# An attention and feed-forward block: each tile's chain spread over three loop periods, with the 32-column matmul groups of three tiles placed in a row

## Chip, cores and metric

The kernel runs on one core of a Trainium2 chip. The metric is the device time of one execution in microseconds. Before the change the median of three runs is 1268.93 us (1268.37 to 1269.41).

## What is computed

The input x is 128 sequences of 32 positions with 512 features, all f32. In the reference's own words, cut to what matters:

```python
def _L0_cond_ref(x, condition, weights):           # one 32x32 matrix per sequence
    return jnp.einsum('bct,bcd->bdt', x, weights[condition])

def _L0_attn_ref(h, w_qkv, q_ln_w, q_ln_b, k_ln_w, k_ln_b, w_out):   # 32 heads of 16
    qkv = jnp.clip(jnp.einsum('bsd,ed->bse', h, w_qkv), -8, 8)
    q, k, v = jnp.split(qkv, 3, axis=-1)
    q, k = _layer_norm(q, q_ln_w, q_ln_b), _layer_norm(k, k_ln_w, k_ln_b)
    ...
    scores = jnp.where(causal, scores * HEAD_DIM ** -0.5 + alibi_bias, -jnp.inf)
    attn = jnp.einsum('bhqk,bkhd->bqhd', jax.nn.softmax(scores, axis=-1), v)
    return jnp.einsum('bsd,ed->bse', attn, w_out)

def _L0_cond2_ref(x, weight, adapter_ids):         # one 512x512 adapter per sequence
    return jnp.einsum('bsi,boi->bso', x, weight[adapter_ids])

def _L0_ffn_ref(h, gate_w, up_w, down_w, fc1_w, fc2_w, expert_w, ln_gamma, ln_beta):
    routing, _ = jax.lax.top_k(h @ gate_w, 2)
    shared = (jax.nn.relu(h @ up_w) ** 2) @ down_w
    routed = (((h @ fc1_w) @ expert_w) * routing.sum(-1, keepdims=True)) @ fc2_w
    return _layernorm(shared + routed, ln_gamma, ln_beta)

x = x + _L0_attn_ref(_L0_cond_ref(x, ...), ...)
x = x + _L0_ffn_ref(_L0_cond2_ref(x, ...), ...)
```

The scale of the scores, the bias and the mask are folded together in the second function; nothing else is.

## The kernel before

The 4096 rows are cut into 32 tiles of 128 rows, four sequences each. Tiles go two by two (`GRP = 2`) through the wide layers of the feed-forward part, since their weights are then loaded into the array once for 256 columns. All weights but the adapters stay on chip. The routed experts' three matrices are multiplied together once, in the prologue (`routed_inner`, `routed_outer`).

A tile t goes through these steps. The name in brackets is how the profile calls the result.

- `load`: x[t] by DMA from SP, and the rows of its conditioning matrices (cw) by an indirect DMA from GpSimd. `load_adapters`: eight DMAs of 512 KB from SP (adw), into a pool of eight buffers, so those of tile t wait until the matmuls of tile t-1 have read theirs.
- `mix`: GpSimd spreads cw into a block-diagonal matrix (blk, L205); four matmuls apply it (pxc, L213); ScalarE copies the result (xcT, L218).
- `project(t, i)`: q, k or v (pqkv, L230), four matmuls of 512 columns each; VectorE clips it and takes the statistics of q and k (L236 to L243).
- `normalise`: ScalarE's square root, then VectorE (L153, L155, L249). `turn`: q and k are transposed. Tiles 0 to 3 do it on TensorE (`flat`, pt, L291); all others (`swap`) by VectorE's transpose in 32x32 blocks (blocks_qk, L272), one DMA to DRAM (away_qk) and four back (T_qk). `scale`: ScalarE applies the norms' weights to k and q (L312, L326) and VectorE spreads k over the heads (kx, L316).
- `scores`: matmuls with 64 rows and 32 columns of the array (psc, L340); VectorE adds the bias (s, L347). `exponent`: VectorE's maximum, GpSimd's subtraction, ScalarE's exp (L357, L358, L363). `share`: sum, reciprocal, and GpSimd's product (L368 to L371). `flip`: VectorE transposes the weights (pT, L379).
- `spread`: GpSimd lays v out per sequence (vx, L390). `weigh`: matmuls with 32 columns of the array (po, L403); VectorE transposes (aT, L414). `attend`: the output projection (pw, L423), added to x (L427).
- `turn_x`: x transposed. Tiles 0 to 2 do it on TensorE with a ScalarE copy (pt_x, L434), all others by `swap`. `adapt`: matmuls with 32 columns of the array (pad, L453); VectorE writes the pair's hT (L458).
- `route(t, half)`: the gate and the merged routed experts (pr, L472), scaled on ScalarE (y, L483, L485) by the sum of the two best gates (top, gs, VectorE).
- `up(g, f)`: eight per pair (pu, L492), ScalarE's relu (act, L497), squared by GpSimd (L498). `down(t, quarter)`: four per tile (pd, L506). `total`, `finish`: the sum, the layer norm and the second residual, then the store.

The main loop runs over periods t. In an even period the eight calls of `fill` are the `up`s of the pair before; in an odd one they are the `down`s of its two tiles. Around them, in the order of the code, one period holds: mix(t+1), scores(t), exponent(t), the projections of q and k of t+1 with share(t) and flip(t) between, normalise and turn of t+1, two or three fills with route(t-2, 0), weigh(t), route(t-2, 1), attend(t), turn_x(t), the projection of v of t+1, the other fills with spread(t+1) and scale(t+1), and adapt(t) last. So a tile's chain lies in two periods: the projections in one, and all from the scores to the adapters in the next.

This order is written by hand, but it is not the queues' order in every place. TensorE's queue holds it as written. On the other engines the framework that builds the program lays the instructions down by when it expects their operands: in the trace, the ScalarE part of scale(t+1) stands ahead of that of finish, which comes earlier in the code, and VectorE's kx alternate with the steps of total. Each engine then works its queue in that order. Buffers come from pools: `w1` has one of each kind, `w2` two, `xp` six tiles of x, and all matmul results share eight PSUM banks.

```python
        when(more, mix, t + 1)
        when(here, scores, t)
        when(here, exponent, t)
        ...
        when(here, weigh, t)
        ...
        when(t % GRP, total, g * GRP + 1)
        when(here, adapt, t)
    finish(NTILE - 1)
```

Of the kernel before, what the change touches and what calls it, by code (L numbers as in the profile page):

```python
# [11 lines left out]
F32 = mybir.dt.float32  # L12
# [5 lines left out]
P = 128  # L18
# [23 lines left out]
def adaln_attn_ffn(  # L42
# [27 lines left out]
    def bank(name):  # L70
        return ps.tile([P, 512], F32, tag="ps", name=name)
# [37 lines left out]
    down_sb = const.tile([P, FC, D], F32, name="down_sb")  # L109
    gam_sb = const.tile([P, D], F32, name="gam_sb")  # L110
    bet_sb = const.tile([P, D], F32, name="bet_sb")
    xp = ctx.enter_context(tc.tile_pool(name="xp", bufs=6))
    wp = ctx.enter_context(tc.tile_pool(name="wp", bufs=8))
    w1 = ctx.enter_context(tc.tile_pool(name="w1", bufs=1))
    w2 = ctx.enter_context(tc.tile_pool(name="w2", bufs=2))
# [14 lines left out]
    def routed_inner(l):  # L130
        pe2 = bank(f"pe2_{l}")
        for m in range(LC):
            nc.tensor.matmul(  # L133
                pe2, lhsT=exp_t[:, m, ts(l, P)], rhs=fc2_t[:, m, :],
                start=(m == 0), stop=(m == LC - 1),
            )
        nc.scalar.copy(e2[:, l, :], pe2)
# [20 lines left out]
    def load(t):  # L158
        x_t = xp.tile([P, D], F32, tag="x", name=f"x_{t}")
        nc.sync.dma_start(out=x_t, in_=x[ts(t, P), :])  # L160
        cw = sm.tile([P, S], F32, tag="cw", name=f"cw_{t}")
        nc.gpsimd.indirect_dma_start(
            out=cw,
            out_offset=None,
            in_=cond_w,
            in_offset=bass.IndirectOffsetOnAxis(ap=rows[:, t : t + 1], axis=0),
        )
        tiles[t] = {"x": x_t, "cw": cw}
# [29 lines left out]

    def mix(t):

        s = tiles[t]
        blk = w2.tile([P, SEQ, S], F32, tag="blk", name=f"blk_{t}")
        nc.gpsimd.tensor_tensor(  # L205
            out=blk,
            in0=s["cw"].unsqueeze(1).broadcast_to([P, SEQ, S]),
            in1=m_seq.unsqueeze(2).broadcast_to([P, SEQ, S]),
            op=ALU.mult,
        )  # L210
        pxc = bank(f"pxc_{t}")
        for c in range(DC):
            nc.tensor.matmul(  # L213
                pxc[:, ts(c, P)], lhsT=s["x"][:, ts(c, P)],
                rhs=blk.rearrange("p a b -> p (a b)"), start=True, stop=True,
            )
        s["xcT"] = w1.tile([P, DC, P], F32, tag="xcT", name=f"xcT_{t}")
        nc.scalar.copy(s["xcT"].rearrange("p c n -> p (c n)"), pxc)  # L218

    def project(t, i, chunks=range(DC)):  # L220

        s = tiles[t]
        if chunks[0] == 0:
            if i == 0:
                s["qk"] = w2.tile([P, 2, D], F32, tag="qk", name=f"qk_{t}")
                s["v"] = w2.tile([P, D], F32, tag="v", name=f"v_{t}")
                s["mv"] = sm.tile([P, 2, 2], F32, tag="mv2", name=f"mv_{t}")
            s["pp", i] = bank(f"pqkv_{t}_{i}")
        for c in chunks:
            nc.tensor.matmul(  # L230
                s["pp", i], lhsT=s["xcT"][:, c, :], rhs=wqkv_sb[:, c, ts(i, D)],
                start=(c == 0), stop=(c == DC - 1),
            )
        if chunks[-1] < DC - 1:
            return
        nc.vector.tensor_scalar(  # L236
            out=s["qk"][:, i, :] if i < 2 else s["v"], in0=s["pp", i],
            scalar1=-CLIP, scalar2=CLIP, op0=ALU.max, op1=ALU.min,
        )
        if i < 2:  # L240
            st = sm.tile([P, 6], F32, tag="st", name=f"st_{t}_{i}")
            nc.vector.bn_stats(out=st, in_=s["qk"][:, i, :])
            nc.vector.bn_aggr(out=s["mv"][:, i, :], in_=st)  # L243
# [21 lines left out]
    def swap(srcs, name):  # L265


        n = len(srcs)
        blocks = w1.tile([P, DC, n, DC, S], F32, tag=f"blocks{n}", name=f"blocks_{name}")
        out = (w1 if n == 1 else w2).tile([P, SEQ, n, DC, S], F32, tag=f"T{n}", name=f"T_{name}")  # L270
        for k, src in enumerate(srcs):
            last_flip[:] = [nc.vector.transpose(  # L272
                out=blocks[:, :, k], in_=src.rearrange("p (c i d) -> p i c d", c=DC, i=DC)
            )]
        away = dram.tile([SEQ, S, DC, n * P], F32, tag=f"away{n}", name=f"away_{name}")
        nc.sync.dma_start(
            out=away.rearrange("j d i n -> (j d) (i n)"),
            in_=blocks.rearrange("p i k c n -> p (i k c n)"),
        )
        for i in range(DC):  # L280
            nc.sync.dma_start(
                out=out[ts(i, S)].rearrange("p j k c n -> p j (k c n)"),
                in_=away[:, :, i].rearrange("j d n -> d j n"),
            )
        return out
# [8 lines left out]
    def turn(t):  # L294


        s = tiles[t]
        if t < 2 * GRP:
            s["T"] = w2.tile([P, SEQ, 2, DC, S], F32, tag="T2", name=f"T_qk_{t}")
            s["raw"] = [flat(s["qk"][:, i, :], f"{t}_{i}") for i in range(2)]  # L300
        else:
            s["T"] = swap([s["qk"][:, i, :] for i in range(2)], f"qk_{t}")
            s["raw"] = [s["T"][:, :, i] for i in range(2)]
# [61 lines left out]
    def share(t):  # L365
        s = tiles[t]
        den = sm.tile([P, H], F32, tag="den", name=f"den_{t}")
        nc.vector.tensor_reduce(out=den, in_=s["s"], axis=AX.X, op=ALU.add)  # L368
        rden = sm.tile([P, H], F32, tag="rden", name=f"rden_{t}")
        nc.vector.reciprocal(rden, den)  # L370
        nc.gpsimd.tensor_tensor(  # L371
            out=s["s"], in0=s["s"], in1=rden.unsqueeze(2).broadcast_to([P, H, S]), op=ALU.mult
        )
# [55 lines left out]
    def turn_x(t):  # L429

        s = tiles[t]
        if t <= GRP:
            s["xT"] = w1.tile([P, SEQ, 1, DC, S], F32, tag="T1", name=f"T_x_{t}")[:, :, 0]
            nc.scalar.copy(s["xT"], flat(s["x"], f"{t}_x"))  # L434
        else:
            s["xT"] = swap([s["x"]], f"x_{t}")[:, :, 0]
        nc.gpsimd.tensor_tensor(out=s["x"], in0=s["x"], in1=bet_sb, op=ALU.add)  # L437
# [106 lines left out]
    load(1)  # L544
    for l in range(LC):
        routed_inner(l)
    mix(0)
    for c in range(DC):
        for i in range(2):
# [13 lines left out]
        )  # L563
    load_adapters(0)
    load(3)
    nc.sync.dma_start(out=bet_sb, in_=beta.broadcast_to([P, D]))

    for g in range(DC):
# [21 lines left out]
    routed_outer(3)  # L590
    turn(1)
    project(1, 2)
    share(0)
    mix(2)
    project(2, 0)
# [9 lines left out]
    project(2, 2)  # L605
    turn_x(0)
    turn(2)
    mix(3)
    project(3, 0)
    share(1)  # L610
    adapt(0)
    load_adapters(1)
    nc.sync.dma_start(out=down_sb, in_=down_w.rearrange("(c p) f -> p c f", p=P))
    nc.sync.dma_start(out=gam_sb, in_=gamma.broadcast_to([P, D]))
    flip(1)
    project(3, 1)
    weigh(1)
    spread(2)
    scale(2)
    route(0, 0)  # L620
    attend(1)
    normalise(3)
    route(0, 1)
    turn_x(1)
    turn(3)
    adapt(1)

    def when(ok, step, *args):
        if ok:
            step(*args)  # L630

    for t in range(GRP, NTILE + GRP):
        here, ahead = t < NTILE, t + 1 < NTILE
        g = t // GRP - 1

        def fill(i):
            if t % GRP == 0:
                up(g, i)
            else:
                down(g * GRP + i // 4, i % 4)  # L640

        when(t + 2 < NTILE, load, t + 2)
        when(here, load_adapters, t)
        more = ahead and t > GRP
        when(more, mix, t + 1)
        when(here, scores, t)
        when(here, exponent, t)
        when(t > GRP and t % GRP == 0, finish, t - GRP - 1)
        when(more, project, t + 1, 0)
        when(here, share, t)  # L650
        when(more, project, t + 1, 1)
        when(here, flip, t)
        when(more, normalise, t + 1)
        when(more, turn, t + 1)
        fill(0)
        fill(1)
        when(t > GRP, route, t - GRP, 0)
        fill(2)
        if not more:
            fill(3)  # L660
        if t == GRP:
            fill(4)
            project(t + 1, 2)
        when(here, weigh, t)
        if t == GRP:
            fill(5)
        when(t > GRP, route, t - GRP, 1)
        when(here, attend, t)
        if t == GRP:
            fill(6)  # L670
        when(here, turn_x, t)
        if more:
            project(t + 1, 2)
            fill(3)
        when(t % GRP, total, g * GRP)
        when(t % GRP, finish, g * GRP)
        when(ahead, spread, t + 1)
        if t > GRP:
            fill(4)
        when(ahead, scale, t + 1)  # L680
        if t > GRP:
            fill(5)
            fill(6)
        fill(7)
        when(t % GRP, total, g * GRP + 1)
        when(here, adapt, t)
    finish(NTILE - 1)


# [75 lines left out]
```

## Time and profile before

| what | value |
|---|---|
| median of three runs | 1268.93 us (1268.37 to 1269.41) |
| profiled execution, its own time | 1265.24 us |
| span of its instructions | 1263.5 us |
| granted TensorE clock, mean | 0.999 |
| DMA, mean over the span | 165 GB/s |
| one odd period (575.84 to 614.05 us) | 38.21 us |

The profile is of one execution; its own time lies 3.69 us under the median of the runs. A group's line gives its start, its length, the engine, the line of the code, the operation, the result and its operands, the part of the array that is used (rows * columns) and the shape of one instruction. Every f32 matmul appears as two instructions. A matmul's length overlaps the next one's start, so times of groups are best taken from start to start.

### The profile page before, as it was taken

The numbers are of one execution on the slowest core, as the hardware profiler recorded it, in microseconds if no ns is written. First come the engines' busy times: TensorE is split into PE (matmuls) and PEld (weight loads), VectorE is DVE, ScalarE is ACT, GpSimd is POOL, SyncE is SP. The second block draws the span as 40 slices with busy tenths as digits, with TensorE's granted clock in tenths as the row PEclk, the third lists the DMA queues.
The fourth block names the chain that finished last, engine by engine and source line by source line (L and its number), as shares of the span: only waits on it lengthen the run. The fifth ranks groups of instructions, "written<-read, shape, count | busy, mean of one in ns | idle before, by whom it ended". The sixth has DMA issues, their size and how long they took to land.

```text
span 1263.5 us, 27891 instructions
## 1 busy us (share of the span) xinstructions
PE 1242.6 (98%) x11636; PEld 787.3 (62%) x11636; DVE 718.4 (57%) x1080; ACT 335.0 (27%) x649; POOL 459.8 (36%) x393
## 2 busy tenths in 40 slices
PE   7999999999999999999999999999999999999997
PEld 3467566665756657466575666657566575666664
DVE  1754654756556664655756647565565646557432
ACT  1432232232322323222222322323223232222311
POOL 4435243443423434334442434424324243333320
PEclk9999999999999999999999999999999999999999
DMA  9565354543455443354543545433454533544410
GB/s 311 129 234 217 116 196 168 201 168 116 153 184 201 151 183 131 140 211 165 194 156 110 188 174 195 168 128 146 180 202 153 195 130 124 216 168 168 155 64 17
DMA packets 92516, 208.71 MB, mean 165 GB/s; under 512 B 11621, under 2 KB 41574, under 8 KB 92390
## 3 DMA queue, kind: packets, MB, share of 16 engines
q1 hardware_dynamic: 88278, 197.74, 44.0%
q0 software_dynamic: 3424, 8.39, 1.8%
q8 instruction: 92, 1.51, 0.5%
q10 hardware_dynamic: 688, 0.79, 0.2%
q14 instruction: 34, 0.28, 0.1%
HBM read 176.21 MB, written 30.67 MB: 164 GB/s over the span
## 4 chain that ended last, share of the span: by engine, by line
PE 97%; DVE 1%; ACT 1%; DMA 0%; POOL 0%; issue 0%; ACTq 0%; DVEq 0%; POOLq 0%
PE pqkv L230 26%; PE pu L492 18%; PE pd L506 17%; PE pr L472 9%; PE pad L453 9%; PE pw L423 9%; PE psc L340 3%; PE pxc L213 3%; PE po L403 3%; DMA fc_t<-in_fc_w 0%; PE pe L133 0%; PE pro L143 0%; ACT xcT L218 0%; ACT T_qk L326 0%; POOL s L358 0%; POOL s L371 0%
## 5 line engine op out<-in xcount | busy, mean ns | idle before, releaser
L230 PE MATMUL pqkv<-wqkv_sb,xcT 128*128 128x512 f32 x768 | 343.6, 597 | 2.9 <-ACT xcT L218 2.9
L230 PEld LDWEIGHTS pqkv<-wqkv_sb,xcT 128*128 128x128 f32 x768 | 143.3, 190 | 176.1 <-issue 172.2
L492 PE MATMUL pu<-hT,up_sb 128*128 128x256 f32 x1024 | 229.3, 380 | 0.8 <-DVE hT L458 0.8
L506 PE MATMUL pd<-down_sb,act 128*128 128x512 f32 x512 | 227.7, 593 | 0.0
L492 PEld LDWEIGHTS pu<-hT,up_sb 128*128 128x128 f32 x1024 | 194.6, 190 | 39.9 <-issue 11.9
L316 DVE TENSOR_TENSOR kx<-T_qk,m_half 128x512 f32<-128x512 f32 x128 | 178.2, 1431 | 1.2 <-ACT T_qk L312 1.2
L506 PEld LDWEIGHTS pd<-down_sb,act 128*128 128x128 f32 x512 | 97.4, 190 | 114.5 <-issue 109.8
L390 POOL TENSOR_TENSOR vx<-v,msk 128x1024 f32<-128x1024 f32 x64 | 143.0, 2252 | 67.8 <-DVE v L236 53.7
L437 POOL TENSOR_TENSOR x<-x,bet_sb 128x512 f32<-128x512 f32 x32 | 40.5, 1267 | 265.8 <-DVE blocks_x L272 258.7
L472 PE MATMUL pr<-rout_sb,hT 128*128 128x256 f32 (+1 forms) x512 | 125.8, 389 | 0.0
L453 PEld LDWEIGHTS pad<-adw,T_x 128*32 128x32 f32 x4096 | 109.9, 110 | 17.4 <-issue 16.3
L498 POOL TENSOR_TENSOR act<-act 128x256 f32<-128x256 f32 x128 | 89.6, 712 | 82.9 <-ACT act L497 82.7
L453 PE MATMUL pad<-adw,T_x 128*32 128x128 f32 x4096 | 118.4, 273 | 0.1
L423 PE MATMUL pw<-wout_sb,aT 128*128 128x512 f32 x256 | 115.3, 593 | 0.0
L472 PEld LDWEIGHTS pr<-rout_sb,hT 128*128 128x128 f32 x512 | 94.9, 190 | 23.3 <-issue 8.6
L427 DVE TENSOR_TENSOR x<-x,pw 128x512 f32<-128x512 f32 x32 | 22.0, 688 | 137.7 <-PE pw L423 133.1
L371 POOL TENSOR_TENSOR s<-s,rden 128x1024 f32<-128x1024 f32 x32 | 61.4, 1920 | 101.6 <-DVE rden L370 101.6
L358 POOL TENSOR_TENSOR s<-s,mx 128x1024 f32<-128x1024 f32 x32 | 61.8, 1930 | 92.7 <-DVE mx L357 92.5
L497 ACT ACTIVATE act<-pu 128x256 f32<-128x256 f32 x128 | 48.6, 380 | 165.5 <-PE pu L492 165.5
L423 PEld LDWEIGHTS pw<-wout_sb,aT 128*128 128x128 f32 x256 | 48.6, 190 | 48.0 <-issue 46.1
L458 DVE STREAM_TRANSPOSE hT<-pad 128x512 f32<-128x512 f32 x32 | 22.9, 717 | 93.8 <-PE pad L453 93.8
L312 ACT ACTIVATE T_qk<-T_qk,lnc 128x128 f32<-128x128 f32 x112 | 46.2, 482 | 107.4 <-DMA T_qk<-away_qk 107.4
(65 smaller groups left out, 1063.2 us busy)
## 6 DMA issues: line engine op xcount, KB each, us to landing
adw<-in_adapt_w SPq DMA_DIRECT2D x256, 512.0 KB, 8.5
away_qk<-blocks_qk SPq DMA_DIRECT2D x28, 512.0 KB, 2.6
T_qk<-away_qk SPq DMA_DIRECT2D x112, 128.0 KB, 2.9
x<-in_x SPq DMA_DIRECT2D x32, 256.0 KB, 3.2
out<-y POOLq DMA_DIRECT2D x30, 256.0 KB, 5.3
away_x<-blocks_x SPq DMA_DIRECT2D x29, 256.0 KB, 2.0
T_x<-away_x SPq DMA_DIRECT2D x116, 64.0 KB, 1.9
wqkv_sb<-in_w_qkvT SPq DMA_DIRECT2D x12, 256.0 KB, 6.2
```

The source lines that it names most:

```text
L230: nc.tensor.matmul(s["pp", i], lhsT=s["xcT"][:, c, :], rhs=wqkv_sb[:, c, ts(i, D)], start=(c == 0), stop=(c == DC - 1),)
L316: kx = nc.vector.tensor_tensor(out=s["kx"][:, c], in0=k[:, :, c].unsqueeze(2).broadcast_to([P, SEQ, HQ, S]), in1=m_half.unsqueeze(1).unsqu ...
L358: nc.gpsimd.tensor_tensor(out=s["s"], in0=s["s"], in1=mx.unsqueeze(2).broadcast_to([P, H, S]), op=ALU.subtract,)
L371: nc.gpsimd.tensor_tensor(out=s["s"], in0=s["s"], in1=rden.unsqueeze(2).broadcast_to([P, H, S]), op=ALU.mult)
L390: nc.gpsimd.tensor_tensor(out=vx, in0=s["v"][:, ts(half, D // 2)].rearrange("p (h d) -> p h d", d=HD).unsqueeze(2) .broadcast_to([P, H // ...
L423: nc.tensor.matmul(pw, lhsT=s["aT"][:, g].rearrange("p b q -> p (b q)"), rhs=wout_sb[:, g, :], start=(g == 0), stop=(g == 3),)
L453: nc.tensor.matmul(pad[ts(g, S), ts(j, P)], lhsT=s["xT"][:, j, c], rhs=s["adw"][c // 2][j][:, c % 2, ts(g, P)], start=(c == 0), stop=(c == ...
L472: nc.tensor.matmul(pr[:, :n], lhsT=hT[:, c, ts(t % GRP, P)], rhs=rout_sb[:, c, ROUT[half] : ROUT[half + 1]], start=(c == 0), stop=(c == DC ...
L492: nc.tensor.matmul(pu[:, : GRP * P], lhsT=up_sb[:, c, ts(f, P)], rhs=pair["hT"][:, c, :], start=(c == 0), stop=(c == DC - 1),)
L497: nc.scalar.activation(a, pu[:, : GRP * P], AF.Relu)
L498: nc.gpsimd.tensor_tensor(out=a, in0=a, in1=a, op=ALU.mult)
L506: nc.tensor.matmul(s["pd"], lhsT=pairs[t // GRP]["acts"][f][:, ts(t % GRP, P)], rhs=down_sb[:, f, :], start=(f == 0), stop=(f == FC - 1),)
```

## The change

Every tile's chain now lies in three periods. In period t the loop does, in the order of the code: the adapters of tile t-1, the scores of t+1 and the weighting of v of t, one behind the other; then the softmax of t+1, route(t-2, 0), mix(t+2), one fill, the projections of q and k of t+2, attend(t) and turn_x(t), three fills, the projection of v of t+1, spread(t+1), scale(t+2), route(t-2, 1) and the last four fills. x is loaded three tiles ahead instead of two, and blk is made by a step of its own (`blend`), three tiles ahead. The prologue therefore also does the scores and the softmax of tile 2 and the scaling of tile 3; adapt(1) goes from there into the loop, and adapt(31) from period 31 to period 32. `xp` has seven buffers, xcT two, the transposed q and k (T2) one. Tile 2's x is transposed by `swap` instead of TensorE.

```diff
--- before.py
+++ after.py
@@ -109,7 +109,7 @@
     down_sb = const.tile([P, FC, D], F32, name="down_sb")
     gam_sb = const.tile([P, D], F32, name="gam_sb")
     bet_sb = const.tile([P, D], F32, name="bet_sb")
-    xp = ctx.enter_context(tc.tile_pool(name="xp", bufs=6))
+    xp = ctx.enter_context(tc.tile_pool(name="xp", bufs=7))
     wp = ctx.enter_context(tc.tile_pool(name="wp", bufs=8))
     w1 = ctx.enter_context(tc.tile_pool(name="w1", bufs=1))
     w2 = ctx.enter_context(tc.tile_pool(name="w2", bufs=2))
@@ -198,23 +198,27 @@
 
 
 
-    def mix(t):
-
-        s = tiles[t]
-        blk = w2.tile([P, SEQ, S], F32, tag="blk", name=f"blk_{t}")
+    def blend(t):
+
+        s = tiles[t]
+        s["blk"] = w2.tile([P, SEQ, S], F32, tag="blk", name=f"blk_{t}")
         nc.gpsimd.tensor_tensor(
-            out=blk,
+            out=s["blk"],
             in0=s["cw"].unsqueeze(1).broadcast_to([P, SEQ, S]),
             in1=m_seq.unsqueeze(2).broadcast_to([P, SEQ, S]),
             op=ALU.mult,
         )
+
+    def mix(t):
+
+        s = tiles[t]
         pxc = bank(f"pxc_{t}")
         for c in range(DC):
             nc.tensor.matmul(
                 pxc[:, ts(c, P)], lhsT=s["x"][:, ts(c, P)],
-                rhs=blk.rearrange("p a b -> p (a b)"), start=True, stop=True,
-            )
-        s["xcT"] = w1.tile([P, DC, P], F32, tag="xcT", name=f"xcT_{t}")
+                rhs=s["blk"].rearrange("p a b -> p (a b)"), start=True, stop=True,
+            )
+        s["xcT"] = w2.tile([P, DC, P], F32, tag="xcT", name=f"xcT_{t}")
         nc.scalar.copy(s["xcT"].rearrange("p c n -> p (c n)"), pxc)
 
     def project(t, i, chunks=range(DC)):
@@ -267,7 +271,7 @@
 
         n = len(srcs)
         blocks = w1.tile([P, DC, n, DC, S], F32, tag=f"blocks{n}", name=f"blocks_{name}")
-        out = (w1 if n == 1 else w2).tile([P, SEQ, n, DC, S], F32, tag=f"T{n}", name=f"T_{name}")
+        out = w1.tile([P, SEQ, n, DC, S], F32, tag=f"T{n}", name=f"T_{name}")
         for k, src in enumerate(srcs):
             last_flip[:] = [nc.vector.transpose(
                 out=blocks[:, :, k], in_=src.rearrange("p (c i d) -> p i c d", c=DC, i=DC)
@@ -296,7 +300,7 @@
 
         s = tiles[t]
         if t < 2 * GRP:
-            s["T"] = w2.tile([P, SEQ, 2, DC, S], F32, tag="T2", name=f"T_qk_{t}")
+            s["T"] = w1.tile([P, SEQ, 2, DC, S], F32, tag="T2", name=f"T_qk_{t}")
             s["raw"] = [flat(s["qk"][:, i, :], f"{t}_{i}") for i in range(2)]
         else:
             s["T"] = swap([s["qk"][:, i, :] for i in range(2)], f"qk_{t}")
@@ -429,7 +433,7 @@
     def turn_x(t):
 
         s = tiles[t]
-        if t <= GRP:
+        if t < GRP:
             s["xT"] = w1.tile([P, SEQ, 1, DC, S], F32, tag="T1", name=f"T_x_{t}")[:, :, 0]
             nc.scalar.copy(s["xT"], flat(s["x"], f"{t}_x"))
         else:
@@ -544,6 +548,8 @@
     load(1)
     for l in range(LC):
         routed_inner(l)
+    blend(0)
+    blend(1)
     mix(0)
     for c in range(DC):
         for i in range(2):
@@ -563,6 +569,7 @@
         )
     load_adapters(0)
     load(3)
+    load(4)
     nc.sync.dma_start(out=bet_sb, in_=beta.broadcast_to([P, D]))
 
     for g in range(DC):
@@ -590,6 +597,7 @@
     routed_outer(3)
     turn(1)
     project(1, 2)
+    blend(2)
     share(0)
     mix(2)
     project(2, 0)
@@ -605,32 +613,40 @@
     project(2, 2)
     turn_x(0)
     turn(2)
+    blend(3)
     mix(3)
     project(3, 0)
     share(1)
+    scale(2)
     adapt(0)
     load_adapters(1)
     nc.sync.dma_start(out=down_sb, in_=down_w.rearrange("(c p) f -> p c f", p=P))
     nc.sync.dma_start(out=gam_sb, in_=gamma.broadcast_to([P, D]))
     flip(1)
+    scores(2)
+    exponent(2)
     project(3, 1)
     weigh(1)
     spread(2)
-    scale(2)
+    blend(4)
     route(0, 0)
+    normalise(3)
     attend(1)
-    normalise(3)
+    share(2)
+    turn(3)
+    scale(3)
+    turn_x(1)
+    flip(2)
     route(0, 1)
-    turn_x(1)
-    turn(3)
-    adapt(1)
 
     def when(ok, step, *args):
         if ok:
             step(*args)
 
+
+
     for t in range(GRP, NTILE + GRP):
-        here, ahead = t < NTILE, t + 1 < NTILE
+        here, ahead, two = t < NTILE, t + 1 < NTILE, t + 2 < NTILE
         g = t // GRP - 1
 
         def fill(i):
@@ -639,51 +655,37 @@
             else:
                 down(g * GRP + i // 4, i % 4)
 
-        when(t + 2 < NTILE, load, t + 2)
+        when(t + 3 < NTILE, load, t + 3)
+        when(t <= NTILE, adapt, t - 1)
+        when(ahead, scores, t + 1)
+        when(here, weigh, t)
         when(here, load_adapters, t)
-        more = ahead and t > GRP
-        when(more, mix, t + 1)
-        when(here, scores, t)
-        when(here, exponent, t)
+        when(ahead, exponent, t + 1)
         when(t > GRP and t % GRP == 0, finish, t - GRP - 1)
-        when(more, project, t + 1, 0)
-        when(here, share, t)
-        when(more, project, t + 1, 1)
-        when(here, flip, t)
-        when(more, normalise, t + 1)
-        when(more, turn, t + 1)
+        when(t > GRP, route, t - GRP, 0)
+        when(two, mix, t + 2)
         fill(0)
+        when(two, project, t + 2, 0)
+        when(ahead, share, t + 1)
+        when(two, project, t + 2, 1)
+        when(ahead, flip, t + 1)
+        when(two, normalise, t + 2)
+        when(two, turn, t + 2)
+        when(here, attend, t)
+        when(here, turn_x, t)
         fill(1)
-        when(t > GRP, route, t - GRP, 0)
         fill(2)
-        if not more:
-            fill(3)
-        if t == GRP:
-            fill(4)
-            project(t + 1, 2)
-        when(here, weigh, t)
-        if t == GRP:
-            fill(5)
+        fill(3)
+        when(t % GRP, total, g * GRP)
+        when(ahead, project, t + 1, 2)
+        when(ahead, spread, t + 1)
+        when(t + 3 < NTILE, blend, t + 3)
+        when(t % GRP, finish, g * GRP)
+        when(two, scale, t + 2)
         when(t > GRP, route, t - GRP, 1)
-        when(here, attend, t)
-        if t == GRP:
-            fill(6)
-        when(here, turn_x, t)
-        if more:
-            project(t + 1, 2)
-            fill(3)
-        when(t % GRP, total, g * GRP)
-        when(t % GRP, finish, g * GRP)
-        when(ahead, spread, t + 1)
-        if t > GRP:
-            fill(4)
-        when(ahead, scale, t + 1)
-        if t > GRP:
-            fill(5)
-            fill(6)
-        fill(7)
+        for i in range(4, 8):
+            fill(i)
         when(t % GRP, total, g * GRP + 1)
-        when(here, adapt, t)
     finish(NTILE - 1)
 
 
```

## The prediction, made blind

> **What bounds the kernel.** The page comes first: the engine shares, and the chain that ended last.
>
> ```profile
> PE 1242.6 (98%) x11636; PEld 787.3 (62%) x11636; DVE 718.4 (57%) x1080; ACT 335.0 (27%) x649; POOL 459.8 (36%) x393
> PE 97%; DVE 1%; ACT 1%; DMA 0%; POOL 0%; issue 0%; ACTq 0%; DVEq 0%; POOLq 0%
> ```
>
> TensorE is the chain, so what counts is what its queue holds and where it stands still. Its waits after the first weights have come:
>
> ```profile
> PE pqkv L230 <- ACT xcT L218: 2.9, 4, 0.8
> PE po L403 <- DVE pT L379: 2.0, 1, 2.0
> PE pu L492 <- DVE hT L458: 0.8, 1, 0.8
> ```
>
> All are in the prologue or the last periods (the timeline has the last two at 1203.7 and 1221.8 us). From 89 to 1191 us TensorE is busy 1101.86 of 1102.00 us, in periods of 38.2 us (odd t) and 38.3 us (even t). But "busy" is not "streaming": matmul ends are modelled, so I read from start to start. One period of TensorE's timeline (start, us, then the group; each f32 matmul counts twice):
>
> ```profile
> 575.84 3.70 PE L453 MATMUL pad<-adw,T_x 128*32 128x128 f32 x128
> 579.47 1.16 PE L213 MATMUL pxc<-blk,x 128*128 128x128 f32 x8
> 580.56 1.16 PE L340 MATMUL psc<-kx,T_qk 64*32 64x128 f32 x64
> 581.65 7.13 PE L230 MATMUL pqkv<-wqkv_sb,xcT 128*128 128x512 f32 x16
> 588.62 3.60 PE L506 MATMUL pd<-down_sb,act 128*128 128x512 f32 x8
> 592.05 1.94 PE L472 MATMUL pr<-rout_sb,hT 128*128 128x264 f32 x8
> 593.83 1.88 PE L506 MATMUL pd<-down_sb,act 128*128 128x512 f32 x4
> 595.64 1.10 PE L403 MATMUL po<-vx,pT 128*32 128x64 f32 x64
> 596.67 2.00 PE L472 MATMUL pr<-rout_sb,hT 128*128 128x256 f32 x8
> 598.50 3.60 PE L423 MATMUL pw<-wout_sb,aT 128*128 128x512 f32 x8
> ```
>
> Eight full-array passes of 512 columns take 3.43 us (588.62 to 592.05), 0.429 each. Around the groups that use 32 columns (pad, psc, po) time is lost:
> - **Into** one: four pd passes should take 1.72 us, but po starts 1.81 after them: 0.09.
> - **Out of** one: 16 pqkv passes after psc take 6.97 us instead of 6.87: 0.10. Eight pr passes of 256 columns after po take 1.83 (596.67 to 598.50); eight of 264 among their like take 1.78, so 1.73 was due: 0.10.
> - pxc, between two of them, takes 1.09 us and bears both losses. Without such neighbours eight passes of 128 take 0.87, as the next view shows (65.88 to 66.75): 0.22.
>
> So each stretch of 32-column work costs 0.20 us for going in and out. A period has three stretches: pad, psc, po.
>
> **The change: TensorE.** At the head of a period now stand pad(t-1), psc(t+1), po(t) in a row. What does going from one tiling to another cost? The trace has it, in the prologue and at t = 2:
>
> ```profile
> 38.40 1.16 PE L340 MATMUL psc<-kx,T_qk 64*32 64x128 f32 x64
> 39.48 3.64 PE L143 MATMUL pro<-e,fc_t 128*32 128x512 f32 x32
> ...
> 65.88 1.04 PE L291 MATMUL pt<-ident,qk 128*128 128x128 f32 x8
> 66.75 1.06 PE L213 MATMUL pxc<-blk,x 128*128 128x128 f32 x8
> ...
> 88.97 3.70 PE L453 MATMUL pad<-adw,T_x 128*32 128x128 f32 x128
> 92.60 1.16 PE L340 MATMUL psc<-kx,T_qk 64*32 64x128 f32 x64
> ```
>
> pad to psc is 3.63 us, as pad to pxc is (575.84 to 579.47); psc to pro is 1.08, as psc to pqkv is 1.09. Each group so keeps its length whatever follows; only the full-array neighbours get shorter. A joined stretch saves one 0.20 for each join.
>
> The Trainium skill speaks here ("TensorEngine Tiling (Array Packing)", Key Properties): changing the tiling mode drains TensorE. pad and po are 128*32, psc is 64*32, so three in a row still change mode four times instead of six: two drains of 0.09 to 0.10 us fewer, 58 x 0.095 = 5.5 us over the kernel. The row says more: the first full-array pass after a stretch is itself 0.1 late, and that goes as well. I take the row.
>
> Count from pad(0) on. Before: pad(0); po(1); pad(1)+psc(2), which join already; po(2); three in each of the 28 periods t = 3 to 30; pad(30)+psc(31); po(31); pad(31): 91. After: pad(0)+psc(2); po(1); one in each of the 30 periods t = 2 to 31; pad(31): 33. **58 fewer x 0.20 = 11.7 us.** The period becomes 37.8 and 37.9 us.
>
> **Last periods.** Before, t = 31 runs tile 31's softmax, weighting, attend and adapters with no projections as cover. The pd group at 1198.13 should lead to po after 3.53 us; po starts after 5.60: 2.1 lost. pad(31) to pu takes 4.53 instead of 3.63: 0.9. Small ones at pw and pad(31): 0.2. After, softmax(31) is done at t = 30, and adapt(31) stands at the head of t = 32, a projection-free period but some 14 us after attend(31): pad(31) needs only x add, transposes and 5.3 us of DMA (blocks_x ends at 527.1, the last T_x is issued at 530.5 and lands 1.9 after). **-3.2 us.**
>
> **Tile 2's turn_x** goes by DMA: four TensorE transposes less (0.44 us), **-0.4 us**; its DMA is covered like every later tile's.
>
> **Prologue.** scale(2), scores(2), exponent(2), share(2), flip(2), scale(3) come earlier. T_qk(2) and kx(2) already ran at 66.6 to 72.7 us, before the place of psc(2) at 75.9: free. kx(3) must be ready by psc(3), at some 93.7. pt(3) ends near 88; VectorE then has x add, four kx (0.6 to 1.4), share and flip, 7 to 10 us of work. Bounds 0 to 3 us late; I take **+1.0**, nearer the low end since share and flip can come before 88. load(4), 256 KB earlier on SP, delays bet, gate and up_w by about 1 us; up is first used after 97 us: nothing.
>
> **The moved steps, in a period from T0 = start of pad.** TensorE: pad 0, psc 3.63, po 4.72, pr0 5.75, pxc 7.58, fill0 8.47, pqkv0 10.19, pqkv1 13.62, pw 17.05, fill1-3 20.48, pqkv2 25.64, pr1 29.07, fill4-7 30.79, next pad 37.8.
> - **xcT is the tight one.** VectorE: two s adds 4.95 to 6.25, aT to 6.95, max to 8.2, top and gs to 8.55. ScalarE: y(pr0) 8.6 to 9.1, xcT (pxc ends about 8.7) to 9.7. pqkv0 is due at 10.19: 0.45 us of slack, given by fill0 alone. Cost: nothing while that holds.
> - Softmax(t+1) then has until the next head for what took 13 us: exp 11.3, pT about 17.
> - q and k of tile t+2: pqkv1 ends 17.05, transposes about 21.6, T_qk lands 8.0 later as now (518.92 to 526.91), k on ScalarE, four kx of 1.43: about 36.5. psc is due at 41.4: 5 us of cover.
> - attend(t): aT at 7, pw at 17. x add and transposes to 23, T_x by 32, pad at 37.8.
> - vx: v at 29.9, two of 2.25, POOL ends 34.5; po due at 42.5.
> - SP queue: x load (its buffer, tile t-4's, is free by then; seven buffers for seven live tiles), eight adapter DMAs freed by pad(t-1), away_qk, four T_qk, away_x, four T_x. Adapters have 34 us for 8.5. Behind a late x load would stand T_qk, which has the 5 us. T2 with one buffer waits for psc(t+1), done at 4.8.
> - POOL: blend is 0.4 us, a period ahead of its mix; the cw gather goes with load.
>
> **Sum** against the profiled execution's own 1265.24 (span 1263.5, 1.74 around it): -11.7 - 3.2 - 0.4 + 1.0 = -14.3: 1250.9. The median of runs stands 3.69 above that execution: **1254.6**.
>
> **Rivals.** (1) *exp ahead of xcT on ScalarE, slower.* exponent(t+1) comes before mix(t+2) in the code. ScalarE and VectorE are strict FIFO ("TensorE: Matmul & The Clock Gate", Architectural detail), and the trace shows what a wrong order costs:
>
> ```profile
> 564.25 1.65 ACT L312 ACTIVATE T_qk<-T_qk,lnc 128x128 f32<-128x128 f32 x4 [3.33 <-DMA T_qk<-away_qk]
> 565.80 0.48 ACT L326 ACTIVATE T_qk<-T_qk,qaff 128x128 f32<-128x128 f32 x1
> 569.04 0.38 ACT L497 ACTIVATE act<-pu 128x256 f32<-128x256 f32 x1 [2.76 <-PE pu L492]
> ```
>
> act was put ahead of three ready T_qk and held them 2.76 us. If xcT stands behind exp: exp ready 10.2, done 11.25, xcT 11.85, pqkv0 at 11.92: 1.73 late in 28 periods, +48: 1303. By code order all of it; by readiness none. The rows favour readiness: scale runs before the older finish (T_qk at 526.9, std_f at 536.3), and at t = 2 exp stands behind two acts although it is earlier in the code. xcT is ready 1.5 us before exp. It decides the sign at 14.3/28 = 0.5 us a period. 14%.
> (2) *Part of the gain.* gs, y or xcT come late by the small slack: 0.3 us x 28 = 8: 1263. The drain-only rule gives 1260.8. 14%.
> (3) *The gaps stay*, each tiling change costing in and out: only the tail's and prologue's -2.6: 1266.3, at the edge of no change. psc to pro and pad to psc speak against it. 4%.
> (4) *kx late*: acts put ahead of T_qk on ScalarE in even periods push kx past 41.4, up to 3 us in 14 periods: 1297 at worst. The 5 us speak against it. 6%.
>
> **Chances.** The forecast has 62%, its own range 1251 to 1259 (prologue 0 to 3, loss per stretch 0.19 to 0.21, 2 us of spread between executions). Half a share of (3) and (4)'s mild cases lie within 0.2% or little beyond. The range 1250 to 1272 holds all but (1) and most of (4). Faster 0.77, same 0.04, slower 0.19; 0.2% is about what this kernel's measurement can tell from nothing.
>
> **What would show it.** Right: start of pad to start of pad near 37.8 us; pad, psc, po adjacent with 3.63, 1.09, 1.03 between starts; pxc 0.87; pqkv0 without a wait for xcT; no wait of po or pu in the last periods. Wrong: a recurring wait of pqkv for xcT (with exp just before it on ScalarE), or of psc for kx or T_qk.

## The result

The changed kernel takes 1330.28 us (median of six runs, 1322.31 to 1334.54) against 1268.48 us (1268.14 to 1269.41, six runs) before: **4.8% slower**, ratio 1.0478, 95% interval 1.0442 to 1.0513. The forecast was 1254.6, faster. Its runs also spread over 12 us, where those of the kernel before lie within 1.3. The profiled execution has a span of 1331.1 us, 67.6 more than before.

The page of the changed kernel: engine shares, the granted TensorE clock in tenths, the queue that carries instructions, and the chain that ended last.

```profile
PE 1259.6 (95%) x11632; PEld 803.3 (60%) x11632; DVE 663.3 (50%) x1081; ACT 329.4 (25%) x648; POOL 424.7 (32%) x393
PEclk9999999998999999999999999999999988999999
q8 instruction: 92, 1.51, 0.5%
PE 92%; issue 4%; DVE 1%; ACT 1%; POOL 1%; DMA 0%; ACTq 0%; POOLq 0%; DVEq 0%
```

TensorE still is the chain, but 4% of the span is now "issue": time in which it waited for nothing that the profile knows. TensorE's waits (engine, line, released by; us in total, times, longest):

```profile
PE po L407 <- issue: 26.9, 13, 3.4
...
PE pr L476 <- issue: 7.6, 2, 3.8
PE pqkv L234 <- ACT xcT L222: 6.7, 8, 1.0
PE pxc L217 <- issue: 5.5, 2, 2.9
PE pu L496 <- issue: 3.4, 2, 2.1
PE psc L344 <- issue: 3.2, 2, 1.7
PE pd L510 <- issue: 1.8, 1, 1.8
PE pw L427 <- DVE aT L418: 1.0, 1, 1.0
```

The "issue" rows add up to 48.4 us, and they sit in po, in what follows it and, twice, in psc. One of these pauses in TensorE's timeline:

```profile
494.42 3.70 PE L457 MATMUL pad<-adw,T_x 128*32 128x128 f32 x128
498.05 1.16 PE L344 MATMUL psc<-kx,T_qk 64*32 64x128 f32 x64
499.13 0.75 PE L407 MATMUL po<-vx,pT 128*32 128x64 f32 x37
502.42 1.06 PE L407 MATMUL po<-vx,pT 128*32 128x64 f32 x27 [2.53 <-issue]
503.41 3.10 PE L476 MATMUL pr<-rout_sb,hT 128*128 128x264 f32 x8
```

po stops after 37 of its 64 matmuls, in the middle of a group whose first half had run on the same operands. pr then takes 2.9 us from start to start instead of 1.9, since the clock has been halved. The profile's clock stands at half for 53.0 us, in windows of 3.4 us or two of them in a row. The last 5.2 us of that come after TensorE's last matmul, as do all the 5.3 us of the kernel before; so 47.8 us are new. A stretch right after the pause that ends at 106.0 us shows one (busy time and count of each engine, then the granted clock, the DMA engines' share and GB/s):

```profile
106.50:110.00 3.50, 3.50 (x6) 1.58 (x6) 1.22 (x1) 2.61 (x3) 0.66 (x2) 0.55 1.03 411
```

What arrives during the pause at 499.9 to 502.4 us is an instruction fetch. The DMA traffic from 500.2 to 501.2 us (queue, kind: packets, MB, share) has one of 16 KB:

```profile
q8 instruction: 1, 0.02, 5.8%
```

Read from the trace's records: 20 pauses of more than 0.9 us have no releaser, and each ends 1.2 to 1.5 us after such a fetch has ended. They also stand where a block of instructions ends. Counted over TensorE's weight loads, matmuls and semaphore instructions, all 20 begin at the same place in a block of 256: 194 instructions and a whole number of blocks from the first. There are 92 fetches for 23,264 weight loads and matmuls and 259 other instructions, 256 to a fetch. The Trainium skill ("Runtime: NRT & Kernel Launch", Instruction fetch mechanics) states blocks of 16 KiB or 256 instructions, the next fetched while the current one executes, and a cost that is mostly hidden. The size agrees. That it stays hidden is not what this trace shows.

Where no pause falls, a period is near what was forecast. An odd one, 37.94 us long:

```profile
700.68 3.70 PE L457 MATMUL pad<-adw,T_x 128*32 128x128 f32 x128
704.31 1.28 PE L344 MATMUL psc<-kx,T_qk 64*32 64x128 f32 x64
705.53 1.10 PE L407 MATMUL po<-vx,pT 128*32 128x64 f32 x64
706.56 2.05 PE L476 MATMUL pr<-rout_sb,hT 128*128 128x264 f32 x8
708.44 1.05 PE L217 MATMUL pxc<-blk,x 128*128 128x128 f32 x8
709.33 3.60 PE L510 MATMUL pd<-down_sb,act 128*128 128x512 f32 x8
712.77 7.03 PE L234 MATMUL pqkv<-wqkv_sb,xcT 128*128 128x512 f32 x16
...
738.62 0.65 PE L457 MATMUL pad<-adw,T_x 128*32 128x128 f32 x16
```

pad, psc and po follow each other at 3.63, 1.22 and 1.03 us, and pxc is down to 0.89. The best odd periods are 37.81 us, 0.39 under the 38.20 of before.

So the theory after the result, **A**: a matmul pass of pad, psc and po is two instructions (a weight load and a matmul) in 27, 14 and 15 ns. The row is 512 instructions in some 5.8 us, two whole fetches, and TensorE runs dry. The rival, **B**: something in the new order costs the time, such as ScalarE's exp, which stands ahead of xcT in every period.

### The profile page after: what moved, and what is told of

Read it like the earlier page. It is cut to its first block, busy times and chain, and to the rows that moved or that the text cites. A ratio compares the mean times of both kernels' runs of the same rounds, so it can differ in the third digit from the quotient of the medians.

```text
span 1331.1 us, 27893 instructions
## 1 busy us (share of the span) xinstructions
PE 1259.6 (95%) x11632; PEld 803.3 (60%) x11632; DVE 663.3 (50%) x1081; ACT 329.4 (25%) x648; POOL 424.7 (32%) x393
## 4 chain that ended last, share of the span: by engine, by line
PE 92%; issue 4%; DVE 1%; ACT 1%; POOL 1%; DMA 0%; ACTq 0%; POOLq 0%; DVEq 0%
PE pqkv L234 25%; PE pd L510 17%; PE pu L496 17%; PE pr L476 9%; PE pad L457 9%; PE pw L427 8%; PE psc L344 3%; PE po L407 2%; PE pxc L217 2%; POOL s L362 1%; PE pe L133 0%; DMA fc_t<-in_fc_w 0%; DVE s L351 0%; DVE mx L361 0%; ACT xcT L222 0%
## 5 line engine op out<-in xcount | busy, mean ns | idle before, releaser
L496 PEld LDWEIGHTS pu<-hT,up_sb 128*128 128x128 f32 x1024 | 194.8, 191 | 36.7 <-issue 11.4
L320 DVE TENSOR_TENSOR kx<-T_qk,m_half 128x512 f32<-128x512 f32 x128 | 92.9, 783 | 120.6 <-ACT T_qk L316 120.6
L502 POOL TENSOR_TENSOR act<-act 128x256 f32<-128x256 f32 x128 | 77.9, 613 | 217.4 <-ACT act L501 217.4
L476 PE MATMUL pr<-rout_sb,hT 128*128 128x256 f32 (+1 forms) x512 | 136.8, 413 | 7.6 <-issue 7.6
L394 POOL TENSOR_TENSOR vx<-v,msk 128x1024 f32<-128x1024 f32 x64 | 119.9, 1897 | 64.3 <-DVE v L240 58.7
L476 PEld LDWEIGHTS pr<-rout_sb,hT 128*128 128x128 f32 x512 | 100.8, 202 | 39.3 <-issue 23.2
L367 ACT ACTIVATE s<-s 128x1024 f32<-128x1024 f32 x32 | 33.9, 1058 | 210.7 <-POOL s L362 210.7
L240 DVE TENSOR_SCALAR qk<-pqkv 128x512 f32<-128x512 f32 x64 | 43.7, 682 | 77.9 <-PE pqkv L234 77.4
L383 DVE STREAM_TRANSPOSE pT<-s 128x1024 f32<-128x1024 f32 x32 | 39.8, 1244 | 78.6 <-POOL s L375 78.6
L153 ACT ACTIVATE std_qk<-mv,eps 128x2 f32<-128x2 f32 x32 | 9.5, 298 | 241.7 <-DVE mv L247 241.6
```

Of the source, the lines that this page charges most:

```text
L240: nc.vector.tensor_scalar(out=s["qk"][:, i, :] if i < 2 else s["v"], in0=s["pp", i], scalar1=-CLIP, scalar2=CLIP, op0=ALU.max, op1=ALU.min,)
L320: kx = nc.vector.tensor_tensor(out=s["kx"][:, c], in0=k[:, :, c].unsqueeze(2).broadcast_to([P, SEQ, HQ, S]), in1=m_half.unsqueeze(1).unsqu ...
L394: nc.gpsimd.tensor_tensor(out=vx, in0=s["v"][:, ts(half, D // 2)].rearrange("p (h d) -> p h d", d=HD).unsqueeze(2) .broadcast_to([P, H // ...
L476: nc.tensor.matmul(pr[:, :n], lhsT=hT[:, c, ts(t % GRP, P)], rhs=rout_sb[:, c, ROUT[half] : ROUT[half + 1]], start=(c == 0), stop=(c == DC ...
L496: nc.tensor.matmul(pu[:, : GRP * P], lhsT=up_sb[:, c, ts(f, P)], rhs=pair["hT"][:, c, :], start=(c == 0), stop=(c == DC - 1),)
L502: nc.gpsimd.tensor_tensor(out=a, in0=a, in1=a, op=ALU.mult)
```

## The experiments

**e1: weigh(t) apart, just before attend(t).**

```diff
         when(ahead, scores, t + 1)
-        when(here, weigh, t)
...
+        when(here, weigh, t)
         when(here, attend, t)
```

> The changed kernel with weigh(t) moved from the head of the period to just before attend(t). Theory A (TensorE runs out of fetched instructions: pad, psc and po are 512 short instructions in 5.4 us): a row of 384 is left and po has full-array work around it, so the pauses inside po, pr and pxc mostly go: 1258 to 1280 us, fewer than 10 us of pauses. Theory B (the loss comes from ScalarE's exp ahead of xcT, or from the chain spread over three periods): it stays, 1315 us or more.

Measured: 1306.64 us (1304.98 to 1309.14), ratio 1.0300 (1.0283 to 1.0317). Neither range holds it. Its waits say why:

```profile
PE pw L427 <- DVE rstd_qk L155: 33.3, 14, 2.4
...
PE psc L344 <- issue: 5.3, 4, 1.9
```

The "issue" pauses fall from 48.4 to 5.9 us, as A expects; but the new place has no cover: pw follows po at once, and aT, its operand, stands on VectorE behind the softmax's transpose and the statistics (the row names rstd_qk, the short step right behind aT). That wait is this experiment's own, in the even periods alone; the odd ones are 38.01 us. It called for e5.

**e2: exp(t+1) ordered behind xcT(t+2), the row kept.**

```diff
+        if t > GRP and t + 1 < NTILE:
+            after(e, tiles[t + 1]["xc"])
...
-        when(ahead, exponent, t + 1)
...
         when(two, mix, t + 2)
+        when(ahead, exponent, t + 1)
```

> The changed kernel with ScalarE's exp(t+1) ordered behind the copy xcT(t+2); the row stays as it is. Theory A (instruction fetch): only the waits of pqkv for xcT go, about 7 us, 1315 to 1330 us. Theory B (exp ahead of xcT is the main loss): below 1290 us.

Measured: 1327.87 us (1322.36 to 1334.91), ratio 1.0457 (1.0428 to 1.0486). As A expects. The waits for xcT go back to the prologue's, the pauses stay:

```profile
PE po L409 <- issue: 28.7, 13, 4.8
...
PE pqkv L234 <- ACT xcT L222: 3.0, 5, 0.8
```

**e3 and e8: the kernel before, with the matmuls of scores issued twice and four times.** The order of the work is the old one; only short instructions are added.

```diff
-        for c in range(DC):
...
+        for _ in range(2):          # e8: range(4)
+            for c in range(DC):
...
```

> The kernel before with every matmul of scores issued twice in a row (the same result is written twice), so that pad, pxc and psc are some 530 instructions in 6.3 us. The additional matmuls themselves cost 32 x 64 x 14.1 ns = 28.9 us. Theory A (instruction fetch): pauses without a releaser appear in most periods and bring clock drops with them, 1310 to 1350 us. Theory B (something in the chain's new order): only the matmuls' own time, 1295 to 1301 us.

> The kernel before with every matmul of scores issued four times (two more than in the run with twice). The additional matmuls themselves cost 32 x 128 x 14.1 ns = 57.8 us over that run's 1343.5. Theory A: beyond the buffered instructions the fetch sets the pace, about 5 us for 256 instructions by the spacing of the fetches, so two more times cost about 5 us a period: 1343.5 + 32 x 5 = 1500 us (1440 to 1520). If fetch does not set the pace: about 1401 us.

Measured: 1343.51 us (1336.35 to 1348.48) and 1605.90 us (1604.54 to 1607.27), ratios 1.0592 (1.0548 to 1.0636) and 1.2667 (1.2641 to 1.2692). e3 is in A's range. The doubled scores cost 75.8 us where their matmuls take 28.9; the next 256 instructions a period cost 262 us, 8.2 a period, where theirs take 1.8. e8 is above A's range as well as far from B's 1401: I had left the clock out. TensorE's waits of e3, then of e8:

```profile
PE psc L341 <- issue: 27.6, 17, 3.0
```

```profile
PE psc L341 <- issue: 157.2, 48, 6.5
```

The clock stands at half for 207.6 us in e8, for 19.6 in e3. The 262 are 130 us of further pauses, half of the further 188 us at half clock and the matmuls' own 58, less 22 that are counted twice, since TensorE stood still in 45 us of e8's half clock (1 in e3): 260. All 44 pauses of psc over 0.9 us end 1.2 to 1.6 us after a fetch. e3 has 16 fetches more than the kernel before and e8 48, for 4,096 and 12,288 instructions more: 256 each. The cause so is the number of short instructions within a few us, and not the order of the changed kernel.

In e8 TensorE often stops twice in one group, exactly 128 weight loads (256 instructions) apart. Two such pairs, and the stretch from the first pause's end to the start of the next fetch, as a window (the last three columns are the granted clock, the DMA engines' share and GB/s):

```profile
73.24 2.02 PE L341 MATMUL psc<-kx,T_qk 64*32 64x128 f32 x128 [0.82 <-issue]
76.96 0.63 PE L341 MATMUL psc<-kx,T_qk 64*32 64x128 f32 x21 [1.71 <-issue]
...
350.79 2.02 PE L341 MATMUL psc<-kx,T_qk 64*32 64x128 f32 x128 [1.83 <-issue]
356.98 0.37 PE L341 MATMUL psc<-kx,T_qk 64*32 64x128 f32 x1 [4.18 <-issue]
```

```profile
73.24:74.38 1.14, 1.14 (x84) 1.14 (x89) 1.14 (x2) 0.23 (x1) 0.90 (x1) 1.00 0.00 0
350.79:354.50 3.71, 2.01 (x128) 1.76 (x128) 0.69 (x1) 0.00 (x0) 0.00 (x0) 1.00 1.04 412
```

From end to end of such a pair it is 3.7 us here, in the prologue, where no other DMA runs, and 5.9 to 6.8 us in the other 14, which run beside the adapter loads. That is what 256 instructions took to come: 15 ns each in the first case, 23 to 26 in the others.

**e4: the adapter loads moved away from the row.**

```diff
-        when(here, load_adapters, t)
...
         when(here, attend, t)
+        when(here, load_adapters, t)
```

> The changed kernel with load_adapters(t) moved from the head of the period to behind attend(t), so that the eight 512 KB loads no longer run while the row is on. Theory A1 (the fetch itself is too slow for the row, whatever else the DMA engines do): 1315 to 1340 us. Theory A2 (the fetches are late because they share the DMA engines with the adapter loads): below 1295 us.

Measured: 1326.61 us (1318.43 to 1332.45), ratio 1.0458 (1.0407 to 1.0509), in A1's range, with the same pauses. But the edit moved nothing. The framework has laid the loads down where it had them before: the first of them is issued 0.7 us after the start of pad in all 26 middle periods of both traces. One of e4's, from TensorE's and SP's timelines:

```profile
694.88 3.70 PE L457 MATMUL pad<-adw,T_x 128*32 128x128 f32 x128
...
695.59 5.10 SPq L190 DMA_DIRECT2D adw<-in_adapt_w  x8
```

So e4 is the changed kernel once more and decides nothing between A1 and A2. The traces speak for a part of A2. Over all runs, after pauses of more than 0.9 us: where the DMA engines are under 20% busy in the microsecond after a pause's end, the next fetch starts 1.1 to 1.3 us after it (12 of 12). Where they are over 90% busy, it starts 2.0 us or later in 121 of 126 cases, 3.65 in the median. The transfer itself takes about 1 us in both. TensorE still runs dry without other DMA (e8's two pauses above, and one of 1.0 us in e3), so the loads are not the whole cause. As an estimate from e8: a block of psc and po is used up in some 2.1 us, so a pause could reach 5.9 - 2.1 = 3.8 us or more beside the loads (3.8 is the changed kernel's longest), and 3.7 - 2.1 = 1.6 without. What the changed kernel would take with its loads elsewhere was not measured.

**e5: weigh(t) between the projections of q and k.**

```diff
-        when(here, weigh, t)
...
         when(ahead, share, t + 1)
+        when(here, weigh, t)
         when(two, project, t + 2, 1)
```

> The changed kernel with weigh(t) between the projections of q and k of tile t+2, so that po stands alone and VectorE's aT has 3.4 us of cover before pw. Theory A (instruction fetch is the whole loss): the clean period of the kernel with weigh before attend, 38.01 us, in nearly all periods, and no wait of pw: 1258 to 1266 us, faster than before. Theory B (the three-period chain costs something else that the pauses hide): above 1270 us.

Measured: 1264.71 us (1263.45 to 1268.92, eight runs) against 1268.13, ratio 0.9981 (0.9969 to 0.9993). Within A's range, near its top, since the prologue is later than I had it. The main waits, without that for the first weights:

```profile
PE pqkv L234 <- ACT xcT L222: 2.8, 4, 0.8
PE psc L344 <- issue: 2.5, 2, 1.3
PE pw L427 <- DVE aT L418: 1.8, 2, 1.0
PE pr L476 <- issue: 1.3, 2, 0.9
```

Moving one group of 128 instructions by 8 us takes 66 us off the changed kernel.

**e6: all three groups apart, the chain still over three periods.** From e5, with scores and exponent behind mix(t+2).

```diff
         when(two, mix, t + 2)
+        when(ahead, scores, t + 1)
+        when(ahead, exponent, t + 1)
         fill(0)
```

> As the one with weigh between the projections, and scores and exponent moved behind mix(t+2): pad, psc and po stand apart as in the kernel before, only the chain is spread over three periods. Theory A: periods of 38.2 us and no pauses; the last periods' 3.2 us and tile 2's 0.4 us are gained: 1262 to 1267 us. If the spread chain itself costs time: 1270 us or more.

Measured: 1266.13 us (1264.88 to 1267.23, 12 runs), ratio 0.9986 (0.9977 to 0.9995). As expected: nearly all periods 38.20 or 38.28 us, one pause, in the prologue. The spread chain by itself costs nothing.

**e7: pad apart, psc and po in a row behind fill(0).**

```diff
         fill(0)
+        when(ahead, scores, t + 1)
+        when(here, weigh, t)
+        when(ahead, exponent, t + 1)
```

> The changed kernel with scores and weigh, still one behind the other, moved behind fill(0): pad alone (256 instructions in 3.4 us), 4.4 us of full-array work, then psc and po (256 in 2.0 us). If what counts is how many instructions come within a few us, this is 512 in 9.8 us and pauses are rare and short: 1258 to 1275 us. If the pace of the single group counts (7.8 ns an instruction): pauses as in the changed kernel, above 1300 us.

Measured: 1269.51 us (1265.63 to 1275.76, 20 runs), ratio 1.0011 (1.0001 to 1.0021). The first of the two: five pauses, of 2.1 us at most and 5.1 us in all, where the row of three had them in most periods. 256 instructions in 2 us are survived if full-array work comes before them.

**e9: e5 with tile 2's scores later in the prologue.**

```diff
     flip(1)
-    scores(2)
-    exponent(2)
     project(3, 1)
...
     route(0, 0)
+    scores(2)
+    exponent(2)
```

> The kernel with weigh between the projections, and in the prologue scores(2) and exponent(2) moved from behind flip(1) to behind route(0, 0), so that psc(2) no longer follows pad(0) at once and VectorE's aT(1) no longer stands behind tile 2's softmax. If the 3.8 us by which the prologue is late (psc 1.6 to 2.0 without a releaser, pw 1.15 for aT, pt_x 0.6, pad 0.4) come from that place: 2 to 4 us under the 1264.7 us of that kernel, 1260.5 to 1263. If they only move: 1264 to 1266.

Measured: 1267.01 us (13 runs, 1264.66 to 1268.92), ratio 0.9995 (0.9986 to 1.0003). A miss: pauses and aT's wait are gone from the prologue, but the time comes back in front of pad(1), which now waits for T_x on ScalarE:

```profile
PE pad L457 <- ACT T_x L438: 3.4, 1, 3.4
```

**e10: the row kept, with half of pad left out.**

```diff
-            for c in range(DC):
+            for c in (0, DC - 1):
                 for g in range(DC):
```

> The changed kernel, the row of pad, psc and po as it is, but with half of the adapters' contraction left out (two of the four chunks of features), so that the row is 384 instructions and 3.7 us instead of 512 and 5.4. The matmuls left out are worth 32 x 64 x 27 ns = 55 us: 1275 us if nothing else changes. Theory A (number of instructions in the row): most pauses and clock drops go too, 1195 to 1230 us. If a row of three tilings, or this order of the work, is itself the cause: 1262 to 1280 us.

Measured: 1241.69 us (1238.98 to 1249.34), between B's 1262 and A's 1230: a miss for both. The waits:

```profile
PE pqkv L234 <- ACT xcT L222: 18.0, 14, 1.8
...
PE pr L476 <- issue: 6.7, 2, 3.6
PE po L407 <- issue: 6.6, 6, 1.9
PE pxc L217 <- issue: 3.5, 2, 1.8
PE pu L496 <- issue: 1.3, 2, 1.1
```

The pauses fall from 48.4 to 18.1 us and the half clock before TensorE's last matmul from 47.8 to 10.2, with the same three tilings in the same order, so it is the count of instructions; 384 in 4 us are still too many in a third of the periods. There are 16 fetches fewer than before, for 4,096 instructions fewer. And with shorter pauses the second fault comes out: exp ahead of xcT, 15 us more than the prologue's share. (With half the contraction left out this kernel's result is not the block's; its time alone is used.)

## Why the prediction was wrong

**The step that failed is "Each group so keeps its length whatever follows".** It was taken from joins of two groups, at single places: pad with psc (384 instructions), psc with pro. The row of 512 does not keep its length. Counted over 27 periods (pad(2) to pad(29)), the kernel before takes 1033.6 us and the changed one 1095.4. Without pauses it would be 1022.0 (37.81 in an odd period; 37.90 in an even one, taken as 38.29 less the same 0.39), so 11.5 us are gained there, as forecast. On top of that come 43.9 us of pauses, 20.0 of clock (half of the 40 us at half clock in which TensorE did not stand still), 3.9 of waits for xcT, and 5.6 in stops too short for the rows of waits, 0.2 a period. The other 5.8 of the 67.6 us lie before and after: 4.5 more of pauses, half of 3.4 us at half clock, and the prologue's waits, less the gains there. (A slip of the sum is small: 58 x 0.20 is 11.6.)

The cause was in no rival, although the kernel before has it in small. In its period that begins at 499.10 us psc is 0.25 us longer than its like: its weight loads stop after 54 and go on with 10, 1.4 us after the end of a fetch.

```profile
503.82 0.81 PEld L340 LDWEIGHTS psc<-kx,T_qk 64*32 64x32 f32 x54
504.79 0.17 PEld L340 LDWEIGHTS psc<-kx,T_qk 64*32 64x32 f32 x10 [0.17 <-issue]
```

Pad's 256 instructions in 3.6 us come faster than the 5.9 to 6.8 us in which e8 got a block beside the loads, so the old order too lived on what had been fetched before. It was at the limit: eight times TensorE came to a block's first instruction 1.4 to 1.8 us after its transfer, and pauses end after 1.2 to 1.6. The change took away the slow full-array groups between.

Point by point:
- *0.20 us for each stretch*: right. One join less or more is 0.19 to 0.20 a period (38.20, 38.01 in e5, 37.81 for odd periods without a pause). The drain-only rule, 0.10, was too low.
- *Last periods, -3.2 us*: about right. No wait of po or pu is left there; from pad(30) to the end e6 takes 70.8 us, the kernel before 75.4, of which 1.1 is psc(31) that moved out: 3.5. Against that, pw waits 0.8 us for aT in period 30 (e5, e6).
- *Tile 2's x by DMA*: no wait for it; not measured alone.
- *Prologue, +1.0*: mis-sized, and in another place. psc(3), which I looked at, came on time. psc(2) behind pad(0) paused 1.3 (e5, e6) to 1.7 us for instructions, pw waited 1.0 for aT, which stands behind tile 2's softmax on VectorE, pt_x and pad(1) 0.4 and 0.3: 3.0 to 3.5 us. e9 shows that it can't be had by moving tile 2's scores alone.
- *Rival 1, exp ahead of xcT*: it happened, in every period, and so my reading that order goes by readiness was wrong here. Its price was 3.8 us and not 48. Where no pause falls, exp ends 10.5 us after pad's start and xcT 11.4, in odd and even periods alike. In an odd period pqkv is not due before 12.0: the lines of 709.33 and 712.77 have two quarters of down (x8) ahead of it, where the code has one, so TensorE's own queue was not as written either. In an even one it is due at 10.2 and waits 1.0 us, unless a pause behind psc has held pqkv back anyway; so it shows in four periods only. e10 and e2 say the same from both sides. One of the four:

```profile
670.03 1.89 PE L496 MATMUL pu<-hT,up_sb 128*128 128x256 f32 x8
672.94 7.13 PE L234 MATMUL pqkv<-wqkv_sb,xcT 128*128 128x512 f32 x16 [1.01 <-ACT xcT L222]
```

- *q, k, kx, vx, T_x, the SP queue*: right, no wait for any of them in the loop.

## What to carry to other kernels

Count instructions, and not only time: in e8 TensorE got 256 instructions in 3.7 us with the other DMA still and in 5.9 to 6.8 us beside the adapter loads, 15 to 26 ns each, while a pass on 32 columns used two in 14 to 27 ns. Long full-array matmuls between short groups are what lets the fetch catch up. So joining short groups to save a mode change (0.20 us each) cost six times what it saved here: 73 us against 11.5 over the 27 periods. The clock adds to it: each of the nine pauses over 2.5 us in the changed kernel was followed by 3.4 or 6.8 us at half clock, and none of those under 2 us was. A wait put down to "issue" in the middle of a group, with a transfer on the instruction queue in it, is the sign. And look in the trace whether an edit has moved what it was to move: e4's had not.

## What was not expected of the hardware

- Pauses end 1.2 to 1.6 us after the fetch's transfer has ended (20 of 20 in the changed kernel, 44 of 44 of psc in e8), and the next fetch starts later beside other DMA: 3.65 us after a pause's end in the median, against 1.1 to 1.3.
- Where a pause falls is fixed by the count of instructions: all 140 pauses over 0.9 us without a releaser, in eleven runs, begin at instruction 193 or 194 of a block of 256. The ends of the blocks drift through the row from period to period, so five periods of the changed kernel's loop are under 38.1 us and others reach 44. That the same program's runs spread over 12 us is not explained by this.
- 48 us of pauses came with 48 us more at half clock, which is half of that again in time, less where pause and half clock overlap (4.4 us).
